# A graph layer on one core: dst broadcast out of SBUF, register loads behind seven columns, fifty double groups without gathers

## The chip, the core and the metric

The kernel runs on one core of one Trainium2 chip. The metric is device time in microseconds of one execution. The kernel before was timed in 13 runs: median 5648.04 us, lowest 5639.12, highest 5659.31. A separate execution was taken with the hardware profiler.

The engines appear under short names: PE is the matrix engine (PEld its weight loads), DVE the vector engine, ACT the scalar engine, POOL the general engine, SP the one that only issues DMAs. Each has a sequencer that reads its instructions in program order. Work of the sequencer itself (register loads, semaphore waits, issuing DMAs) is marked with a q, as in DVEq.

## The reference

One layer of a graph network over 12500 nodes with 128 features and 400000 edges, which are sorted by their destination dst:

```
h   = max(layernorm(x), 0)
m   = relu(concat(h[src], h[dst], edge_attr) @ w1 + b1) @ w2 + b2
agg = segment_sum(m, dst)
out = x + GRU(agg, h)          # gates r, z, n from agg @ w_ih and h @ w_hh
```

All is f32. The heavy part is 400000 rows h[src], taken at random, and a sum by dst.

## The kernel before, in words

**Tables.** A first phase (lines 210 to 337) normalizes x, keeps h transposed in SBUF as hT_all (128 features x 12500 nodes) and writes A = h @ w1[0:128] to DRAM. So an edge needs one row of A, and what depends on dst and the edge's attributes is added by matmuls.

**Units.** The edges come in 3125 tiles of 128. Eight tiles are a double group k (391 of them, 1024 edges each); half of one is a unit u = 2k or 2k+1 (782). All dst of a double group lie in two windows of V = 32 nodes each, since dst is sorted. The main loop (line 932) goes over units, and everything is written out by hand in the order in which each engine is to run it (manual_schedule), with later units' first stages ahead of earlier units' last ones: `stages(u)` (line 896) makes the one-hot of unit u + 6 or so, the matmuls `pre` of unit u + 3, the `add` (L630, DVE) and `relu` (L636, ACT) of unit u + 2, and `seg(u)` (L649, PE) sums unit u by window. Other lines of the loop that matter below, all on DVE: `take` L657 copies a finished sum, `onehot_T` L503 compares the broadcast dst (tile Ld) with the nodes of the window, `window` L522 copies a window's columns of hT_all, `window_rows` L539 adds two windows' rows after PE's L530, and `onehot` L557 makes the one-hot for `seg`.

**Three ways to A's rows.** For most double groups POOL issues eight indirect DMAs (`gather`, L148), each of 128 rows of 512 bytes, into a buffer G. There are GBUFS = 7 buffers after the first stage; the gathers for a later double group are issued when the relu of the second unit has freed one (`gathers`, line 876). The other double groups are "by hand" (SPREAD, line 48): 21 are copied by DVE and 20 by ACT, column by column, out of hT_all (L816 and L814, 128 partitions x 4 bytes each, at an address in a register), and then go through w1 on PE (L616) so that there is no add on DVE; 6 are copied by SP, row by row, from A in DRAM with one DMA of 512 bytes a row (L821). So 1024 columns or rows make one such double group.

**How a job by hand is spread.** `Job` (line 785) loads 32 registers at once (L801, LOAD = 32) with the places of the next 32 columns. DVE and ACT do so once a unit, in `behind` (line 839), which stands right after the add on DVE and right after the relu on ACT: there it runs the columns that are left, TAIL = 9 of them, then loads the next 32 registers. The rest is spread over the four calls of `run_jobs` in the loop, which leave TAIL: with 32 - 9 = 23 columns these are 6, 6 and 6 in phases 1, 2 and 3 of this unit and 5 in phase 0 of the next. Phase 0 stands before `stages`; L539 is issued after phase 3 of an even unit, L557 in `stages` of the odd unit, ahead of its add. A job of DVE or ACT takes at least 32 units (an assert), and jobs of one engine come one after the other over the loop. SP spreads its 1024 DMAs evenly over the units of a job, and its next job begins only when the double group of the last one has been used.

**SP's queue** holds besides these rows the broadcast of dst (`fetch_d`, L496), the edge attributes (`fetch`, L487), index tiles and the nodes' loads and stores. `fetch_d(q)` serves two double groups (QP = 2) and is issued at the head of unit 4q - 12, if one of three buffers of Ld is free.

Of the kernel before, what the change touches and what calls it, by code (L numbers as in the profile page):

```python
# [8 lines left out]
F32 = mybir.dt.float32  # L9
F16 = mybir.dt.float16  # L10
I32 = mybir.dt.int32
# [13 lines left out]
NP = T // PAIR + 1  # L25
NU = 2 * NP

V = 32
# [6 lines left out]
QP = 2  # L35
# [8 lines left out]
CH = PLACE * PAIR  # L44
LOAD = 32

TAIL = 9
SPREAD = {"dve": 21, "act": 20, "sp": 6}
NR = 12672

H_AT = 16512
# [6 lines left out]
def tile_gnn(ctx: ExitStack, tc: tile.TileContext, x, src, srcT, dstT, dstP, eaT, eaP, w1, b1, w2T, b2,  # L58
             wih, bih, whh, bhh, out):
    nc = tc.nc  # L60
# [8 lines left out]
    ge = early.enter_context(tc.tile_pool(name="ge", bufs=EARLY, side="right"))  # L69
# [15 lines left out]

    mode, order = {}, {m: [] for m in SPREAD}
    for m, n in SPREAD.items():
        lo, hi = {"dve": (JOBS0 + 3, NP - 14), "act": (JOBS0 + 11, NP - 6),
                  "sp": (JOBS0 + 5, NP - 10)}[m]
        for i in range(n):  # L90
            k = lo + int((i + 1) * (hi - lo) / n)
# [47 lines left out]
    def gather(k):  # L139
        if k >= NP or k in mode:  # L140
            return
        pool = ge if early_pair(k) else gp
        G[k] = pool.tile([128, GRP, 2, D], F32, name="G")
        table = x if k < RAW else A
        for u in (2 * k, 2 * k + 1):
            for t, j, a in unit_tiles(u):
                c, i = divmod(t, CH)
                nc.gpsimd.indirect_dma_start(  # L148
                    out=G[k][:, j, a, :], out_offset=None, in_=table,
                    in_offset=bass.IndirectOffsetOnAxis(ap=src_i[c][:, i:i + 1], axis=0))  # L150
# [61 lines left out]
    with tc.tile_pool(name="pp", bufs=3) as pp:  # L212
# [69 lines left out]
        def chunk(q):  # L282
            b, c = chunks[q]
            i0, n = bats[b]
            return b, i0, c, min(n, c + 4), PB(b), (i0 + c) * 128
# [3 lines left out]
        for q in range(NC + 3):  # L289
            if q < NC:  # L290
                b, i0, c, e, P, n0 = chunk(q)
# [3 lines left out]
            if 1 <= q <= NC:  # L295
                b, i0, c, e, P, n0 = chunk(q - 1)
# [6 lines left out]
            if q >= 3:  # L303
                b, i0, c, e, P, n0 = chunk(q - 3)
# [4 lines left out]
            if q < NC:  # L309
                b, i0, c, e, P, n0 = chunk(q)  # L310
# [4 lines left out]
            if 1 <= q <= NC:  # L315
                b, i0, c, e, P, n0 = chunk(q - 1)
# [3 lines left out]
            if q >= 3:  # L320
                b, i0, c, e, P, n0 = chunk(q - 3)
                if e == bats[b][1]:
                    nc.sync.dma_start(nodes(A, i0, e, P), asb[b][:P, :e, :])
            if 2 <= q <= NC + 1:
                b, i0, c, e, P, n0 = chunk(q - 2)
# [13 lines left out]
    p3 = ctx.enter_context(tc.tile_pool(name="p3", bufs=3, reuse_waits="tile"))  # L339
# [138 lines left out]
    Ls, Ds, OH, RT, HE, SEG = ({} for _ in range(6))  # L478
    hand = {}

    def fetch(q):
        if q * QP >= NP:
            return
        n = min(QP, NP - q * QP)
        c = slice(q * QP * 512, (q * QP + n) * 512)
        Ls[q] = p3.tile([128, QP * 512], F32, name="L")
        nc.sync.dma_start(Ls[q][2 * V:, :n * 512], eaP[:, c])  # L487

    def fetch_d(q):
        if q * QP >= NP:  # L490
            return
        n = min(QP, NP - q * QP)
        c = slice(q * QP * 512, (q * QP + n) * 512)
        Ds[q] = p3.tile([2 * V, QP * 512], I32, name="Ld")
        for a in range(2):
            nc.sync.dma_start(Ds[q][V * a:V * (a + 1), :n * 512],  # L496
                              dstP[a:a + 1, c].to_broadcast([V, n * 512]))

    def onehot_T(k):
        if k >= NP:  # L500
# [59 lines left out]
    def unit(u):  # L560
        k, h = divmod(u, 2)
        return G[k][:, 2 * h:2 * h + 2, :, :].rearrange("p j a f -> p (j a) f")


    def slots(u):
        return [(j % 2) * 2 + a for _, j, a in unit_tiles(u)]
# [18 lines left out]
    def raw_turn(u):  # L585
        if u < 2 * RAW:
            l = slots(u)
            pt = ps1.tile([128, 512], F32, name="misc")
            for i, s in enumerate(l):
                nc.tensor.transpose(pt[:, i * 128:(i + 1) * 128], unit(u)[:, s, :], ident)  # L590
            hT = p3.tile([128, 512], F32, name="hTe", bufs=2)
            nc.vector.tensor_copy(hT[:, :len(l) * 128], pt[:, :len(l) * 128])
            HE[u] = hT

# [258 lines left out]
    def run_jobs(u, phase):  # L853
# [3 lines left out]
        for m in ("act", "dve"):  # L857
            if m in live:
                n = max(0, len(live[m].vals) - TAIL)
                live[m].run(TAIL + n - -(-n // (4 - PARTS.index(phase))))  # L860
        if phase == 0:
# [14 lines left out]
    def gathers(u):  # L876
        while asked[0] < NP and (asked[0] in mode or 2 * taker[asked[0]] + 1 < u + 2):
            gather(asked[0])
            asked[0] += 1
# [3 lines left out]
            pass  # L883

    gathers(0)
    for q in range(2):
        fetch_d(q)
        fetch(q)
    fetch_d(2)
    for k in range(3):  # L890
        window(k)
# [4 lines left out]
    def stages(u):  # L896
        if u + 7 >= 0:
            raw_stats(u + 7)
        if u + 6 >= 0:
            raw_fin(u + 6)  # L900
            raw_h(u + 6)
        if u % 2 == 0:
            onehot_T(u // 2 + 3)
            if u >= 0:
                window(u // 2 + 3)
        elif u > -7:
            onehot(u // 2 + 3)
        if u + 4 >= 0:
            raw_turn(u + 4)
        if u + 3 >= 0:  # L910
            pre(u + 3)
        if u + 2 >= 0:
            add(u + 2)
            behind("dve", u)
            relu(u + 2)
            behind("act", u)
# [15 lines left out]
    for u in range(NU):  # L932
        k, h = divmod(u, 2)
        gathers(u)
        if h == 0:
            if k % QP == 0:
                fetch_d(k // QP + 3)
                fetch(k // QP + 2)
            if k % BP == 0 and k:
                nodes_left.append([node(k // BP - 1), 0])  # L940
            if k % PLACE == 1:
                indices(k // PLACE + 2)
            if k % PLACE == 5:
                place(k // PLACE + 1)
                dst_tile(k // PLACE + 2)
            if k == NP - 20:
                check_windows()
# [198 lines left out]
```

## Time and profile before

| | us |
|---|---|
| median of 13 runs | 5648.04 |
| lowest, highest | 5639.12, 5659.31 |
| the profiled execution's own time | 5635.89 |
| its span in the trace | 5633.9 |

The first section of the page has busy times and their shares of the span, then the number of instructions:

```profile
PE 3133.0 (56%) x13642; PEld 1881.1 (33%) x13642; DVE 2996.7 (53%) x25579; ACT 2802.7 (50%) x21960; POOL 2626.4 (47%) x2757
```

The queues, with packets, MB and the share of 16 DMA engines' time that the packets took; q0 is POOL's gathers, q1 what SP issues, q14 and q8 the instructions:

```profile
q0 software_dynamic: 87968, 180.33, 12.9%
q1 hardware_dynamic: 68127, 137.35, 8.5%
```

The DMAs that SP issues for dst and the edge attributes, with their number and size:

```profile
Ld<-in_dstP SPq DMA_DIRECT2D x390, 128.0 KB
L<-in_eaP SPq DMA_DIRECT2D x195, 256.0 KB
```

A line of a group of instructions has the source line, engine, operation, out<-in, shapes and number; then busy time and the mean ns of one; then the idle time of the engine just before them and what ended most of it. "issue" there means that no semaphore ended the wait: the sequencer had not got so far. Register loads and DMA issues are not counted as busy. A timeline line has start, length, engine and line; equal instructions that follow one another are merged (x23), and the brackets hold the idle time before the first.

### The profile page before, as it was taken

To read this page: it belongs to the slowest core of one execution; us is meant where nothing else is said; L and a number is where in the kernel's file an instruction comes from. 1 tells how busy PE (TensorE), PEld (TensorE's weight loads), DVE (VectorE), ACT (ScalarE), POOL (GpSimd) and SP (SyncE) were. 2 spreads that over 40 slices of the span, in tenths; PEclk is the share of its full clock that TensorE was granted. 3 is DMA by queue.
4 is the path that set the end of the run, shared out by engine and by line. 5 is a ranking of instruction groups with operands and counts; after the bars stand their busy time and mean duration, and the time that the engine had idled before them with its cause. 6 is when DMAs were issued, how large, how long until landed. Compare 5 with 4: busy or idle time off the path is not lost. (4 is left out here: it accounts for less than half of the span.)

```text
span 5633.9 us, 99560 instructions
## 1 busy us (share of the span) xinstructions
PE 3133.0 (56%) x13642; PEld 1881.1 (33%) x13642; DVE 2996.7 (53%) x25579; ACT 2802.7 (50%) x21960; POOL 2626.4 (47%) x2757
## 2 busy tenths in 40 slices
PE   2665555455556555545655554555555456465557
PEld 2532333333323333323333332333333233233334
DVE  3645555555555555555555555555555555555553
ACT  2413554546454554545455545555454545455454
POOL 5445444444444444454444444453444444444443
PEclk7775666566566666656657665666666666566667
DMA  3322222221222222221222222222222222222221
GB/s 111 82 63 60 56 57 57 57 56 51 58 56 57 57 55 55 53 59 48 57 57 52 58 54 56 55 54 56 54 53 58 56 54 53 58 56 54 58 53 46
DMA packets 156906, 324.15 MB, mean 58 GB/s; under 512 B 64549, under 2 KB 76624, under 8 KB 156239
## 3 DMA queue, kind: packets, MB, share of 16 engines
q0 software_dynamic: 87968, 180.33, 12.9%
q1 hardware_dynamic: 68127, 137.35, 8.5%
q14 instruction: 553, 4.53, 0.3%
q8 instruction: 114, 1.87, 0.1%
q10 hardware_dynamic: 144, 0.07, 0.0%
HBM read 303.66 MB, written 13.84 MB: 56 GB/s over the span
## 5 line engine op out<-in xcount | busy, mean ns | idle before, releaser
L148 POOL DMA_INDIRECT G<-A,src_i x2672 | 2552.4, 955 | 2929.2 <-ACT RB L636 2056.2
L814 ACT COPY HE_act<-hT_all 128x4 uint8 x20480 | 2237.0, 189 | 1583.7 <-issue 1568.6
L816 DVE TENSOR_REDUCE HE_dve<-hT_all 128x4 uint8 x21504 | 1700.6, 147 | 1817.6 <-issue 1807.0
L605 PE MATMUL pre<-RW,L 128*128 128x256 f32 x3128 | 1383.6, 581 | 1376.0 <-DVE G L630 1170.7
L605 PEld LDWEIGHTS pre<-RW,L 128*128 128x128 f32 x3128 | 806.8, 286 | 1758.9 <-issue 1382.0
L636 ACT ACTIVATE RB<-G 128x512 f32<-128x512 f32 x668 | 420.2, 629 | 694.8 <-DVE G L630 350.6
L530 PE MATMUL oh<-w1b,hw 128*64 128x128 f32 x782 | 242.5, 408 | 865.0 <-DVE hw L522 461.3
L649 PE MATMUL seg<-RB,OH 128*32 128x129 f32 x6250 | 704.7, 365 | 10.8 <-ACT RB L636 6.3
L630 DVE TENSOR_TENSOR G<-pre,G 128x512 f32<-128x512 f32 x668 | 456.8, 684 | 58.7 <-issue 45.6
L649 PEld LDWEIGHTS seg<-RB,OH 128*32 128x32 f32 x6250 | 377.6, 140 | 279.8 <-issue 157.7
L530 PEld LDWEIGHTS oh<-w1b,hw 128*64 128x64 f32 x782 | 102.7, 186 | 1075.5 <-DVE hw L522 566.0
L539 DVE TENSOR_TENSOR RW<-oh,b1b 32x128 f32<-32x128 f32 x782 | 217.0, 277 | 311.2 <-issue 209.1
L658 ACT CAST dcol<-seg 64x1 f16<-64x1 f32 x391 | 59.6, 152 | 315.3 <-DVE sums L657 145.0
L657 DVE COPY sums<-seg 64x128 f32<-64x128 f32 x391 | 107.5, 275 | 199.4 <-remote 118.7
L503 DVE TENSOR_SCALAR L<-Ld,node_of 64x512 f32<-64x512 int32 x391 | 186.8, 478 | 2.6 <-issue 2.6
L557 DVE TENSOR_TENSOR OH<-dloc,iota 128x256 f32<-128x256 f16 (+1 forms) x392 | 162.8, 416 | 1.1 <-issue 0.2
L680 PE MATMUL nd<-spot,sums 64*128 64x40 f32 x782 | 157.6, 386 | 1.0 <-issue 1.0
L680 PEld LDWEIGHTS nd<-spot,sums 64*128 64x128 f32 x782 | 153.4, 301 | 12.0 <-issue 12.0
L644 PE MATMUL seg<-zrow 1*64 1x129 bf16 x391 | 114.2, 292 | 0.9 <-remote 0.9
L699 PE MATMUL misc<-DEG,brow 33*128 33x512 f32 x112 | 72.7, 732 | 67.0 <-DVE gt L716 67.0
L328 PE MATMUL pre<-w1a,hT_all 128*128 128x128 f32 x196 | 51.5, 415 | 77.7 <-issue 58.0
L699 PE MATMUL nd<-DEG,brow 33*128 33x512 f32 x112 | 89.0, 886 | 3.8 <-ACT HE_act L814 2.5
(151 smaller groups left out, 1726.9 us busy)
## 6 DMA issues: line engine op xcount, KB each, us to landing
G_sp<-A SPq DMA_DIRECT2D x6144, 0.5 KB
Ld<-in_dstP SPq DMA_DIRECT2D x390, 128.0 KB
L<-in_eaP SPq DMA_DIRECT2D x195, 256.0 KB
G<-A,src_i POOLq DMA_INDIRECT x2672
xb<-in_x SPq DMA_DIRECT2D x28, 256.0 KB
out<-xb SPq DMA_DIRECT2D x28, 256.0 KB
xs<-in_x SPq DMA_DIRECT2D x11, 512.0 KB
A<-asb SPq DMA_DIRECT2D x11, 512.0 KB
```

The costliest lines, as they stand in the source:

```text
L148: nc.gpsimd.indirect_dma_start(out=G[k][:, j, a, :], out_offset=None, in_=table, in_offset=bass.IndirectOffsetOnAxis(ap=src_i[c][:, i:i + ...
L503: nc.vector.tensor_scalar(Ls[k // QP][:2 * V, c], Ds[k // QP][:, c], node_of[:, k:k + 1], None, op0=ALU.is_equal)
L530: nc.tensor.matmul(PB_[k][:2 * V, :D], HW.pop(k).rearrange("p a v -> p (a v)"), w1b, start=True, stop=True)
L539: nc.vector.tensor_tensor(RW[k % 4][s, a, :], pm[s, :D], b1b[s, :], op=ALU.add)
L557: nc.vector.tensor_tensor(o, d.to_broadcast(shape), i.to_broadcast(shape), op=ALU.is_equal)
L605: nc.tensor.matmul(PP[u][:, 2 * i:2 * i + 2, :], Ls[k // QP][:, c0:c0 + 128], RW[k % 4], start=True, stop=not raw)
L630: nc.vector.tensor_tensor(RT[u], PP.pop(u), RT[u], op=ALU.add)
L636: nc.scalar.activation(o[:, :, :D], RT.pop(u), AF.Relu)
L649: nc.tensor.matmul(SEG[k][V * a:V * (a + 1), :D + 1], OH[k][:, j, a, :], RB[u % 3][:, (j % 2) * 2 + a, :D + 1], start=False, stop=all(b != ...
L680: nc.tensor.matmul(pt[:, bass.ds(offs[i], V + SHIFT)], sums[:, i, :], spot, start=False, stop=i == n - 1)
L814: nc.scalar.copy(to[:, e * 4:e * 4 + 4], h_bytes[:, bass.ds(v - H_AT, 4)])
L816: nc.vector.tensor_reduce(to[:, e * 4:e * 4 + 4], h_bytes[:, bass.ds(v - H_AT, 4), None], AX.X, ALU.max)
```

## The change

Three edits, in one diff (its core):

```diff
-TAIL = 9
-SPREAD = {"dve": 21, "act": 20, "sp": 6}
+TAIL = 7
+SPREAD = {"dve": 22, "act": 21, "sp": 7}
...
+    DST = 64
+    dst_s = {}
+
+    def stage_dst(c):
+        n = min(DST, NP - c * DST)
+        if n <= 0:
+            return
+        dst_s[c] = p3.tile([128, 512], I32, name="dst_s", bufs=2)
+        for a in range(2):
+            nc.sync.dma_start(dst_s[c][DST * a:DST * a + n, :],
+                              dstP[a:a + 1, c * DST * 512:(c * DST + n) * 512].rearrange(
+                                  "o (k e) -> (o k) e", e=512))
...
     def fetch_d(q):
         if q * QP >= NP:
             return
-        n = min(QP, NP - q * QP)
-        c = slice(q * QP * 512, (q * QP + n) * 512)
+        if q * QP % DST == DST // 2:
+            stage_dst(q * QP // DST + 1)
         Ds[q] = p3.tile([2 * V, QP * 512], I32, name="Ld")
-        for a in range(2):
-            nc.sync.dma_start(Ds[q][V * a:V * (a + 1), :n * 512],
-                              dstP[a:a + 1, c].to_broadcast([V, n * 512]))
+        for k in range(q * QP, min(NP, (q + 1) * QP)):
+            for a in range(2):
+                r = DST * a + k % DST
+                nc.sync.dma_start(
+                    Ds[q][V * a:V * (a + 1), (k % QP) * 512:(k % QP + 1) * 512],
+                    dst_s[k // DST][r:r + 1, None, :].to_broadcast([1, V, 512]))
...
-            hT = p3.tile([128, 512], F32, name="hTe", bufs=2)
+            hT = ge.tile([128, 512], F32, name="hTe", bufs=2)
...
     gathers(0)
+    stage_dst(0)
```

First, dst of 64 double groups is loaded at a time into a tile of 128 partitions (one half of a double group's dst in each partition, 512 numbers or 2 KB), 32 double groups ahead. The broadcast to 32 partitions then reads one partition of that tile in place of DRAM; it is one DMA of 64 KB for each half of a double group, four for two double groups, where there were two of 128 KB. The tile hTe of the first units moves to another pool, which is closed later on.

Second, nine columns behind the add and the relu become seven, so 25 are left for the four phases: 7, 6 and 6 in phases 1 to 3 and 6 in phase 0.

Third, 22, 21 and 7 double groups are copied by DVE, ACT and SP, 50 in place of 47, and 24 gathers fewer are issued by POOL. The jobs' spans become shorter: 32 or 34 units for most of DVE's (34 before), 34 for ACT's (36 before), and some 94 for SP's (110 before).

## The prediction

> **What bounds the kernel now.** I read the groups first, then a timeline of DVE, ACT and POOL over one pair of units, then the register loads by line, then SP's waits.
>
> ```profile
> L148 POOL DMA_INDIRECT G<-A,src_i x2672 | 2552.4, 955 | 2929.2 <-ACT RB L636 2056.2
> L814 ACT COPY HE_act<-hT_all 128x4 uint8 x20480 | 2237.0, 189 | 1583.7 <-issue 1568.6
> L816 DVE TENSOR_REDUCE HE_dve<-hT_all 128x4 uint8 x21504 | 1700.6, 147 | 1817.6 <-issue 1807.0
> ```
>
> No engine is busy for more than 56% of the span. POOL's largest idle time ends with a relu (L636), which is what frees a G buffer. DVE and ACT idle before their columns for "issue": they wait for nothing that a semaphore shows. The timeline, with lines left out, says what that is:
>
> ```profile
> 3041.95 0.63 ACT L636 ACTIVATE RB<-G 128x512 f32<-128x512 f32 x1
> ...
> 3042.45 1.56 DVE L816 TENSOR_REDUCE HE_dve<-hT_all 128x4 uint8 x23 [0.68 <-issue]
> ...
> 3042.84 0.95 POOL L148 DMA_INDIRECT G<-A,src_i  x1 [5.99 <-ACT RB L636]
> ...
> 3044.62 0.66 DVE L816 TENSOR_REDUCE HE_dve<-hT_all 128x4 uint8 x9
> ...
> 3046.35 0.29 DVE L816 TENSOR_REDUCE HE_dve<-hT_all 128x4 uint8 x3 [1.08 <-issue]
> ...
> 3049.25 0.16 DVE L816 TENSOR_REDUCE HE_dve<-hT_all 128x4 uint8 x1 [0.51 <-issue]
> ...
> 3051.59 0.95 POOL L148 DMA_INDIRECT G<-A,src_i  x1 [0.30 <-issue]
> ...
> 3054.26 0.35 DVE L816 TENSOR_REDUCE HE_dve<-hT_all 128x4 uint8 x4 [0.57 <-issue]
> 3054.52 0.56 DVE L539 TENSOR_TENSOR RW<-oh,b1b 32x128 f32<-32x128 f32 x2
> ```
>
> A relu frees a buffer; 0.9 us later POOL issues eight gathers, 1.25 us apart (0.95 busy and 0.30 between). While their data is on the way, columns that ran 64 ns apart come one or two in 0.7 us, on ACT and SP too, and it ends about 0.5 us after the last gather has landed, which is 1.26 us after POOL's last instruction. Then DVE runs its leftover columns, L539 twice, the columns of phase 0, L557 and the add; ACT does the relu, and the next burst starts. So a pair of units (one double group) with gathers lasts 0.9 + 9.7 + 1.3 + 0.5 us, plus the leftover, plus 2.2 us from L539 to the relu. Sorting the relus by start, 293 pairs with a full burst took 15.0 us in the mean, and 43 pairs without a gather 9.5 us. DVE's program between the end of the slow stretch and the relu sets the end; ACT waits for the add.
>
> Before each stretch of columns stands a load of 32 registers, and it is not cheap:
>
> ```profile
> L801 DVEq TENSOR_LOAD <-at x672: 2097/2122/2834, 358.3 to 5453.8; - x168
> L801 ACTq TENSOR_LOAD <-at x640: 1965/2004/2491, 470.6 to 5558.2; - x160
> ```
>
> The columns issued ahead of it (nine) are what DVE does meanwhile; then it idles 0.89 us in the mean (0.79 on ACT).
>
> **The sum's base.** The profiled execution took 5635.9 us, its span 5633.9; the median of the 13 runs is 5648.0, so I add 12.1 at the end.
>
> **Three more double groups without gathers.** Three pairs go from 15.0 to 9.5 us: -16.5. DVE gets 1024 columns more, in 32 units or 16 pairs, some 14 of them with a burst. There, a pair has 8 leftover columns (mean) and 5 of phase 0 between the slow end and the add: 13 x 64 ns = 0.83 us, x14 = +12; the other columns lie under the burst. ACT gets 16 pairs more with columns. 32 pairs without them took 14.49 us with 7.8 gathers, 259 with them 14.37 with 6.9; at 5.5/8 = 0.69 us a gather that is 0.5 us a pair, x16 = +8. Adds, seven columns' matmuls and the like of three groups are under 5 us on engines that wait; nothing.
>
> SP gets 1024 copies more, 0.32 us apart in calm stretches and 0.56 in the mean, and 32 loads of 2.1: 400 to 640 us. Its waits:
>
> ```profile
> SPq L496 <- DVE hw L522: 435.6, 88, 32.2
> SPq L821 <- ACT RB L636: 90.4, 5, 22.2
> SPq L487 <- PE seg L649: 50.0, 18, 7.3
> ```
>
> With the smaller ones some 700 us are free while jobs run. SP reaches the fetch of a unit about 28 us before DVE reaches that unit, and a landed Ld waits 55 to 75 us for its use. I take nothing for SP; the other end is below.
>
> **Loads behind 7 columns, not 9.** In 307 of the 672 DVE loads (those of odd units) the load starts 22 ns after the add starts, with nine columns still to come, and in 27 others 49 ns after the instruction before L557, with L557 and nine to come: the sequencer could not run further ahead. With two fewer behind it, the odd unit's load should start about when L557 does, 0.42 + 0.03 us before the add. Relative to the add it then starts 0.46 us earlier, but the two columns are done later: -0.46 + 0.13 = -0.33 us to the next unit's L657. In the even unit the load starts 0.12 us after L503 starts, and could start some 0.3 us earlier until the sequencer's own pace (48 ns an instruction) holds it. So that load ends 0.33 us earlier against the burst. What is this worth? Loads that end 3 to 4 us into a burst are followed by 13.5 columns before the first gap, at 4 to 5 us by 8.3, at 5 to 6 us by 5.0: 3.3 to 5.2 columns a us, so 1.1 to 1.7 columns or 0.07 to 0.11 us. Against it stand one more column behind the load (25 in four parts is 7, 6, 6, 6 where 23 was 6, 6, 6, 5) and one more in phase 0: +0.13. Net +0.04 in each of some 270 pairs: +11. In 46 pairs without a burst both loads count, with two columns given back: -0.33 + 0.13 = -0.2 each: -9.
>
> From both sides: if no load starts sooner, two columns lose their cover at each load, 0.26 us a pair, x316 = +81; if all of both gains counted in every pair, -0.66 + 0.19, x270 = -127. I take +2 since the rows of columns after a load are the nearest.
>
> **dst out of SBUF.** Two DMAs for two double groups become four; the two of a staging come once in 64 groups. Issue: L496 takes 0.37 us (median), 390 more are 145 us on SP, in the same free time. DVE's L503 now has up to two more semaphores to wait for: a sequencer wait takes 70 ns of its pace, 196 x 2 x 0.07 = 27 at most, ahead of the even unit's load. I take +7. The first fetch must wait for the staging: some 3 us at 173 us, where the first L503 comes at 186.9 and has no DMA to wait for; nothing. hTe's move changes only where it lies. The transfer: today 128 packets of 2 KB take 0.1 us each on 16 engines. No row reads one partition from 16 engines. Below: the same 0.1 us, and no gain either, since neither gathers (1.26 us to landing, 1.38 at the 95th of 100, with or without Ld) nor L503 wait for it. Above: one engine's row of 512 bytes into one partition is 27 ns, 19 GB/s; if the partition gives only that to all, 64 KB take 3.4 us, four DMAs 14 us of each 28.5, and a packet 1.7 us. A gather packet behind one lands that much later: half of 293 pairs x 1.7 = +249 at most. I take 0: the load is 6 groups ahead of its use and 16 queues' packets overlapped from one DRAM row.
>
> [...]
>
> Sum: -16.5 + 12 + 8 + 11 - 9 + 7 = +12.5, so 5648.4 in the profile and **5660** as a median.
>
> **Rivals.**
> - *The loads are worth more* (faster). If columns saved from the slow stretch also save what stalls behind them, a pair with a burst gains 0.2 us, about half of the bound above: -54 in place of +11, total -52: 5596. For it: 1807 us of "issue" on DVE is the largest idle time. Against: most of it lies under a burst.
> - *dst crowds the gathers* (slower). The partition's 14 us in 28.5 cover a burst's end in half of the pairs, and half a packet, 0.85 us, is the mean delay: 293 x 0.5 x 0.85 = +125, or 5785. It decides from the point where a 2 KB packet takes over 0.5 us. SP's shortage has the same sign: 640 + 67 + 190 against 700 free is up to 200 us, if its new copies fall into slow stretches.
> - *TAIL does not do what it says*: the sequencer is not held by what is queued, and nothing starts earlier: +81 for +2, 5739.
>
> **Chances.** Forecast (the edits cancel, 5640 to 5680) 0.36; loads worth more 0.34; dst or SP late 0.20; no earlier load 0.10. A measurement tells 0.2% (11 us) from nothing. Faster is the first rival and a little of the forecast's own width, 0.38; half of the forecast is within 0.2%, 0.18; slower is the rest, 0.44. The forecast's own range is 5640 to 5680; the range to hold 8 in 10 takes in the first rival and most of the third and cuts the second: 5585 to 5760.
>
> **What would show it.** Pairs with a burst at 15.0 us; DVE's loads starting at L557 rather than the add; the idle time before L816 per load down from 0.89 or up; the Ld packets' time in the queue table; gathers' landing still 1.26 us after POOL's last; SP still waiting at the fetch of dst. I am wrong if pairs with a burst shorten by 0.2 us or more, if landing moves, or if SP's wait is gone and DVE waits at L503.

## The result, and the profile after

The changed kernel took 5907.97 us (median of 8 runs, 5897.48 to 5930.09) where the kernel before took 5647.87 in 37 runs: a ratio of 1.0467, 95% interval 1.0455 to 1.0478, or 260 us more. The forecast was 5660, with 5760 as the upper end.

The changed kernel's page, first the busy time by engine, then the two queues and the DMAs for dst and the edge attributes, then the three groups. Lines of the code lie 16 or 17 further down than before (L496 is now L512, L605 L622, L636 L653, L801 L818, L816 L833, L821 L838).

```profile
PE 3131.1 (53%) x13674; PEld 1878.8 (32%) x13674; DVE 3055.6 (52%) x26599; ACT 2902.0 (49%) x22984; POOL 2614.4 (44%) x2733
...
q1 hardware_dynamic: 89889, 139.52, 17.8%
q0 software_dynamic: 87200, 178.76, 11.6%
...
L148 POOL DMA_INDIRECT G<-A,src_i x2648 | 2540.5, 959 | 3204.8 <-ACT RB L653 2315.8
L831 ACT COPY HE_act<-hT_all 128x4 uint8 x21504 | 2323.0, 189 | 1721.9 <-issue 1697.6
L833 DVE TENSOR_REDUCE HE_dve<-hT_all 128x4 uint8 x22528 | 1765.0, 147 | 2028.3 <-issue 2018.6
...
Ld<-dst_s SPq DMA_DIRECT2D x782, 64.0 KB
L<-in_eaP SPq DMA_DIRECT2D x195, 256.0 KB
```

Busy time hardly moved: DVE has 59 us more, ACT 99, POOL 12 less. The 260 us are waiting. POOL waits 260 us more for a relu, so the pairs became longer: 15.6 us with a burst (15.0 before) and 10.9 without (9.5). Queue q1 moved 1.6% more bytes but its packets took twice the time, 17.8% for 8.5%. The packet records say which: 33294 packets of 2 KB at 393 ns in the mean, 782 x 32 of them the broadcasts out of SBUF. In a fetch with no other 2 KB packets beside it these take 490 ns in the mean: 42% of them 84 ns or little more, 37% over 800 ns, and 99 in 100 under 1.12 us.

SP's waits in the changed kernel (what was waited for, total us, times, longest):

```profile
SPq L512 <- DVE hw L539: 71.6, 11, 23.0
...
SPq L838 <- ACT RB L653: 20.6, 6, 5.2
...
SPq L487 <- PE seg L666: 2.8, 7, 1.0
```

Before, these were 435.6, 90.4 and 50.0. SP's spare time is nearly gone. And PE has a wait in the changed kernel that was not in its list before, the third here:

```profile
PE pre L622 <- DVE G L647: 920.4, 191, 8.9
PE oh L547 <- DVE hw L539: 410.5, 162, 11.3
PE pre L622 <- DMA L<-in_eaP: 402.3, 43, 18.2
```

L is the edge-attribute tile. A timeline of the changed kernel (start, length, engine, line) shows one such wait, all engines in one window, with lines left out:

```profile
3376.20 11.63 SPq L838 DMA_DIRECT2D G_sp<-A  x18
...
3378.75 1.07 PE L666 MATMUL seg<-RB,OH 128*32 128x129 f32 x8
...
3387.92 3.15 SPq L512 DMA_DIRECT2D Ld<-dst_s  x4
...
3391.17 0.54 SPq L487 DMA_DIRECT2D L<-in_eaP  x1
...
3397.09 1.19 PE L622 MATMUL pre<-RW,L 128*128 128x256 f32 x2 [17.26 <-DMA L<-in_eaP]
```

PE has been idle since 3379.8. SP is still issuing rows of its own job, then the four copies of dst, and gets to L at 3391.2; L lands some 5 us later. I followed SP's lead (time from its issue of Ld at the head of a unit to DVE's L520 of that unit) through the run: before it is 27 us in the mean and never under 12; after, it falls in each of the seven SP jobs from some +17 us to between -30 and -45 in about 100 units, 0.6 us a unit, and recovers when the job ends.

So the first theories were: **A**, SP's queue has become the bound; **B**, the copies out of SBUF themselves hold up other transfers; **C**, the shorter TAIL or the added columns cost it.

### The profile page after: what moved, and what is told of

It is laid out like the page before. It is cut to its first block, busy times and chain, and to the rows that moved or that the text cites. A ratio compares the mean times of both kernels' runs of the same rounds, so it can differ in the third digit from the quotient of the medians.

```text
span 5898.6 us, 104372 instructions
## 1 busy us (share of the span) xinstructions
PE 3131.1 (53%) x13674; PEld 1878.8 (32%) x13674; DVE 3055.6 (52%) x26599; ACT 2902.0 (49%) x22984; POOL 2614.4 (44%) x2733
## 3 DMA queue, kind: packets, MB, share of 16 engines
q1 hardware_dynamic: 89889, 139.52, 17.8%
## 5 line engine op out<-in xcount | busy, mean ns | idle before, releaser
L831 ACT COPY HE_act<-hT_all 128x4 uint8 x21504 | 2323.0, 189 | 1721.9 <-issue 1697.6
L833 DVE TENSOR_REDUCE HE_dve<-hT_all 128x4 uint8 x22528 | 1765.0, 147 | 2028.3 <-issue 2018.6
L622 PE MATMUL pre<-RW,L 128*128 128x256 f32 x3128 | 1369.6, 576 | 1570.4 <-DVE G L647 920.4
L622 PEld LDWEIGHTS pre<-RW,L 128*128 128x128 f32 x3128 | 798.8, 283 | 1957.2 <-issue 1637.5
L653 ACT ACTIVATE RB<-G 128x512 f32<-128x512 f32 x662 | 416.4, 629 | 606.2 <-DVE G L647 279.1
L520 DVE TENSOR_SCALAR L<-Ld,node_of 64x512 f32<-64x512 int32 x391 | 187.4, 479 | 5.3 <-issue 5.1
L539 DVE COPY hw<-hT_all 128x64 f32 x391 | 78.9, 202 | 27.6 <-issue 17.2
```

What stands on the lines that cost most here:

```text
L520: nc.vector.tensor_scalar(Ls[k // QP][:2 * V, c], Ds[k // QP][:, c], node_of[:, k:k + 1], None, op0=ALU.is_equal)
L622: nc.tensor.matmul(PP[u][:, 2 * i:2 * i + 2, :], Ls[k // QP][:, c0:c0 + 128], RW[k % 4], start=True, stop=not raw)
L653: nc.scalar.activation(o[:, :, :D], RT.pop(u), AF.Relu)
L831: nc.scalar.copy(to[:, e * 4:e * 4 + 4], h_bytes[:, bass.ds(v - H_AT, 4)])
L833: nc.vector.tensor_reduce(to[:, e * 4:e * 4 + 4], h_bytes[:, bass.ds(v - H_AT, 4), None], AX.X, ALU.max)
```

## The experiments

Each ratio is to the kernel before on the experiment's own chip, with its 95% interval. On those chips the kernel before took 5559 to 5560 us (the first two groups and b_sp1, b_none11), 5637 (b_spread, a_l_act, b_sp5, b_half) and 5622 (a_l4, h_sbuf, b_few, b_act). Names with a_ start from the changed kernel, with b_ from the one before; h_sbuf is b_half with dst out of SBUF.

### One edit taken back

a_sp6: six SP jobs.

```diff
-SPREAD = {"dve": 22, "act": 21, "sp": 7}
+SPREAD = {"dve": 22, "act": 21, "sp": 6}
```

> The changed kernel with six SP jobs in place of seven; dst still comes from SBUF in four DMAs a fetch, and TAIL is 7. Theory A (SP's queue has become the bound: within each SP job it falls behind by about 60 us in 100 units, 0.6 us a unit, and TensorE then waits for L): with 9.3 copies a unit for 11 SP has 1.0 us a unit more, keeps its lead of 15 to 30 us, the wait of L622 on L's DMA (402 us) falls under 60 us, and the time is 5650 to 5720 us. Theory B (the broadcasts out of SBUF themselves, with packets of 393 ns, hold up gathers and L): the packets are as before, so the wait stays above 250 us and the time above 5800 us. Theory C (the shorter TAIL and the longer columns cost it): above 5800 us also, without a wait for L.

Measured 1.0244 (1.0221 to 1.0267). The wait for L is gone and SP's lead is 26 us, as A said; but over half of the loss stays, as A did not.

a_dram2: `fetch_d` as before the change; a_dram4: the same, but in four DMAs, so that only the source differs from the change.

```diff
-                    dst_s[k // DST][r:r + 1, None, :].to_broadcast([1, V, 512]))
+                    dstP[a:a + 1, k * 512:(k + 1) * 512].to_broadcast([V, 512]))
```

> The changed kernel with dst out of DRAM again, in two DMAs of 128 KB a fetch; TAIL 7 and the 22, 21 and 7 jobs stay. Theory A: SP is spared two issues of about 0.85 us in four units, 0.4 us a unit of the 0.6 that it loses, so it still loses ground inside each SP job but little of it reaches TensorE: 5650 to 5740 us, wait for L under 120 us. Theory B: all of the loss goes, 5620 to 5680 us, and SP's lead is as in the kernel before. Theory C: above 5800 us.

> The changed kernel with dst out of DRAM, but in the same four DMAs of 64 KB and packets of 2 KB as the change has; only the source of the copy differs from the changed kernel. Theory A in its form 'number of issues': SP's issues are as many, so SP falls behind as in the changed kernel and the time stays at 5850 to 5930 us. Theory B: packets at about 100 ns in place of 393, so the time falls to 5640 to 5720 us. Halfway, 5740 to 5850 us, would say that the issue of a copy out of SBUF is itself longer on SP.

Measured 1.0176 (1.0159 to 1.0193) and 1.0182 (1.0165 to 1.0199). The number of DMAs costs nothing that can be measured; the source costs some 2.9%. From DRAM the 2 KB packets take 107 ns and an issue 0.36 us of SP (mean), from SBUF 393 ns and 0.68 us.

a_tail9: the changed kernel with TAIL = 9.

> The changed kernel with TAIL 9 again, nothing else. Theories A and B: SP's queue and the broadcasts are as they were, so the time stays within 1% of 5908 us (5850 to 5960 us) and the wait for L at 300 to 500 us. Theory C: the loads in the midst of the columns were the cost, and the time falls below 5780 us.

Measured 1.0488 (1.0460 to 1.0516): C falls for TAIL.

The expectations of these four count in us for a chip on which the kernel before takes 5648. There the four ratios stand for 5786, 5747, 5751 and 5924 us. So a_sp6 lies between A and B, a_dram2 a little above both, a_dram4 in the halfway band (an issue out of SBUF is indeed longer), and a_tail9 where A and B put it. No single theory holds; the rest takes the edits one by one.

### One edit made alone

b_sbuf has the hunks of the change for `stage_dst`, `fetch_d` and hTe, and the constants of before. The other three change a constant of the kernel before each, in the order b_sp7, b_tail7, b_cols:

```diff
-SPREAD = {"dve": 21, "act": 20, "sp": 6}
+SPREAD = {"dve": 21, "act": 20, "sp": 7}
...
-TAIL = 9
+TAIL = 7
...
-SPREAD = {"dve": 21, "act": 20, "sp": 6}
+SPREAD = {"dve": 22, "act": 21, "sp": 6}
```

> The kernel before with one part of the change: dst is copied out of SBUF (with hTe in its other pool, which makes the room), TAIL 9 and 21, 20 and 6 jobs as before. Theory A (the broadcasts cost only SP's time, and only where SP runs out of it): with six SP jobs the changed kernel kept a lead of 26 us, so nothing reaches TensorE, ratio 0.997 to 1.004. Theory B (the broadcasts also hold up the gathers' landing and the L tiles): ratio 1.006 to 1.015, with gathers landing later than 1.26 us after POOL's last instruction in a quarter of the bursts.

> The kernel before with seven SP jobs in place of six, dst out of DRAM, nothing else. Theory A: SP's lead over VectorE falls from 27 to some 10 us on the mean, but never far enough that TensorE waits for L; one pair less has a burst (5.5 us saved), ratio 0.997 to 1.003. Against it: the copies of rows lengthen the pairs by 0.04 to 0.06 us each, some 2.5 more a pair, ratio 1.006 to 1.010.

> The kernel before with TAIL 7 in place of 9, nothing else. The prediction took +2 us, bounds -127 and +81 us. From the changed kernel with 7 and with 9 (1.0467 and 1.0488, intervals that meet): ratio 0.996 to 1.003. If the shorter tail hurts without the rest, 1.005 to 1.015.

> The kernel before with 22 VectorE jobs and 21 ScalarE jobs in place of 21 and 20, six SP jobs, TAIL 9, dst out of DRAM. The prediction's working (two pairs without a burst save 11 us; a tenth more columns cost 20 us): ratio 1.000 to 1.003. Theory D (columns cost more than their busy time, since they and their loads lie in the stretch in which the gathers slow the sequencers): the changed kernel with dst out of DRAM is 1.018 with 7 SP jobs, and most of that is the columns, ratio 1.010 to 1.018.

Measured:

| edit alone | ratio | 95% interval | us |
|---|---|---|---|
| dst out of SBUF | 1.0173 | 1.0146 to 1.0199 | 96 |
| seventh SP job | 1.0111 | 1.0082 to 1.0139 | 62 |
| TAIL 7 | 1.0015 | 0.9999 to 1.0030 | 8 |
| 22 and 21 jobs on DVE and ACT | 1.0075 | 1.0047 to 1.0104 | 42 |

TAIL came as expected. dst out of SBUF and the seventh job lie a little above the upper range of each, the columns between their two ranges. In none of the four does PE wait for L for more than 11 us (b_sp7). SP's lead in b_sp7 is 2.5 us in the mean, but inside a job it falls from 17 us or more to between -10 and -30 (means of five fetches), with dst out of DRAM. So the seventh job alone takes SP out of its time. The three sizable ones add up to 3.6%; the changed kernel with TAIL 9 has just these three, on chips of the same speed, and costs 4.9%. Pairs of edits without that surplus fit the sum: a_sp6 has 2.4 where the parts give 2.6, a_dram2 1.8 where they give 2.0. So the surplus shows only where the SBUF copies and the seventh job meet (always with the added columns too; the two alone were not run).

**Where b_sbuf loses it.** The q1 lines of b_sbuf and a_dram4:

```profile
q1 hardware_dynamic: 87835, 138.98, 18.7%
```

```profile
q1 hardware_dynamic: 88901, 137.92, 8.5%
```

A fetch of 128 packets takes 5.5 us from the first start to the last end in b_sbuf, 2.1 in a_dram4 (medians). I took each burst of eight gathers and asked when its last packet ended after POOL's last instruction. With no L or dst packets near the burst's end, it is 1.24 us in b_sbuf and 1.25 in a_dram4. With them, in 105 of 299 bursts of b_sbuf, 2.21 us in the mean; in a_dram4, 37 bursts, 1.48 us. A third of b_sbuf's bursts land later than 1.5 us (kernel before: 4%). This moves the landing by 0.3 us in the mean, or 90 us over 300 bursts, a little of which comes back, because columns run in the meantime.

### Three mechanisms, tried apart

b_spread: b_sbuf with each row on four partitions, 32 apart (and 16 double groups staged at a time in eight DMAs, 200 in all where the expectation says 100; these lines are left out here).

```diff
-                    dst_s[k // DST][r:r + 1, None, :].to_broadcast([1, V, 512]))
+                    dst_s[k // DST][r:r + 97:32, None, :].to_broadcast([4, V // 4, 512]))
```

> The kernel before with dst copied out of SBUF (TAIL 9, 21, 20 and 6 jobs), but every row lies on four partitions, 32 apart, and each of the same 64 KB copies reads a quarter from each; 16 pairs are staged at a time, 100 stagings in all. Theory B1 (one partition feeds all 32 packets of a copy, so that its 2 KB packets take 391 ns in place of 107, a fetch takes 5.5 us in place of 2.1, and the gathers of a third of the bursts land 1 us later): packets of 100 to 200 ns, landing over 1.5 us in under 15% of the bursts, ratio 1.001 to 1.008. Theory B2 (a copy out of SBUF is slow whatever partition it reads): packets above 330 ns and ratio 1.014 to 1.020, as in the kernel with the single row.

Measured 1.0180 (1.0163 to 1.0197). Packets fell to 111 ns and late landings to 10%, as B1 said, but the time did not follow. The test was not clean: 4 to 6 packets were in flight at a time where b_sbuf has 16 or 17, so a fetch still took 4.6 us; and SP's lead fell to 13 us with the stagings' DMAs. It says that shorter packets alone don't help, and not which partition arrangement would. It also speaks against the landing as the whole cost: its cycles, counted as in the table further down, are 15.4 us where the kernel before, on a chip of the same speed, has 15.1; the landing is 1.35 us (before 1.29), but the next burst comes 4.3 us after it (before 4.0). This loss lies behind the landing, and what makes it is not shown.

a_l_act: the changed kernel with L on ScalarE's queue.

```diff
-        nc.sync.dma_start(Ls[q][2 * V:, :n * 512], eaP[:, c])
+        nc.scalar.dma_start(Ls[q][2 * V:, :n * 512], eaP[:, c])
```

> The changed kernel with the edge-attribute tile L fetched from ScalarE's queue, no longer behind SP's copies; nothing else. Theory A for the part of the loss that the single parts don't give (they add to 3.7%, the change costs 4.7%): L arrives late only because SP issues it late, so the wait of L622 on L's DMA (402 us) falls under 60 us, and the ratio to 1.033 to 1.041. If the transfer of L itself is what is late, the wait stays above 250 us and the ratio above 1.044. ScalarE's own issue of 196 copies is some 0.5 us each, beside its columns.

Measured 1.1073 (1.1036 to 1.1111): neither. By the profile, ACT itself now stood 970 us ahead of its columns (L831) until DMAs that SP issues had ended. It settles nothing on L.

a_l4: L two pairs earlier instead.

```diff
-        Ls[q] = p3.tile([128, QP * 512], F32, name="L")
+        Ls[q] = p3.tile([128, QP * 512], F32, name="L", bufs=4)
...
-                fetch(k // QP + 2)
+                fetch(k // QP + 3)
```

> The changed kernel with L fetched two pairs (some 30 us) earlier into four buffers; the room comes from one buffer of dst_s (staged at the start of its 64 pairs), one of hTe and four of OH in place of six. Theory A (the loss beyond the added parts is TensorE's wait for L, because SP issues it late): the wait of L622 on L's DMA falls from 402 us to under 60, the ratio from 1.047 to 1.033 to 1.041. If the wait goes and the ratio stays at 1.044 or more, the wait for L only took the place of another wait, and SP's lateness reaches the pairs by another way (the rows of G_sp, or dst itself).

Measured 1.0435 (1.0415 to 1.0454). PE's wait for L is gone entirely, but only 0.3% of the time with it (on chips whose speed differs by 0.5%, and with fewer buffers for OH, dst_s and hTe, which may cost something of their own). The instructions on tile Ld in a_l4 say what is late next: DVE's line L520, which compares dst, now stands for it.

```profile
L520 DVE TENSOR_SCALAR L<-Ld,node_of x391: 464/479/717, 186.6 to 5831.8; 64x512 f32<-64x512 int32 x196
its engine sat idle before it (us, times) until:
  DMA Ld<-dst_s: 72.9, 18
```

17 of these 18 waits fall into four stretches of 8 to 12 double groups, where SP's lead is lowest. SP is still 11 us behind DVE in the mean, and whatever it issues is late in turn. The 402 us of waiting were thus worth about 20 us of time; of the rest, 196 us are back as PE's wait for DVE's add, which rose from 920 to 1116.

h_sbuf: dst out of SBUF with 11, 10 and 3 jobs, to be set against b_half below.

> The kernel before with 11, 10 and 3 jobs and dst copied out of SBUF, TAIL 9; to be set against the same with dst out of DRAM (0.9447), in which SP waits 1530 us at the fetch of dst. Theory landing (the 2 KB packets of 391 ns stand ahead of the gathers' last packets; a third of the bursts land 1 us later, some 350 bursts, 0.3 us each, 100 us): ratio 0.957 to 0.966. Theory SP (the copies cost SP's time, which is to spare here): ratio 0.943 to 0.949, with a third of the bursts landing late all the same.

Measured 0.9541 (0.9520 to 0.9563) against 0.9447: 1.0% for the copies, while SP waits over 1200 us at their fetch:

```profile
SPq L512 <- DVE hw L539: 1257.2, 124, 35.3
```

34% of the bursts land later than 1.5 us, 0.26 us in the mean over the cycles below, and these cycles are 0.26 us longer (14.11 to 14.37). The ratio lies between the two expected ranges, but these two numbers agree: where SP has time, the copies cost about what they add to the landing. That is a match of two means; b_spread, which cost as much with few late landings, does not fit it.

### Do pairs by hand pay at all?

b_sp7 and b_cols had asked what one more job costs. These ask what fewer bring. Each is one line of the kernel before, in the order b_sp5, b_half, b_few, b_act, b_sp1:

```diff
-SPREAD = {"dve": 21, "act": 20, "sp": 6}
+SPREAD = {"dve": 21, "act": 20, "sp": 5}
+SPREAD = {"dve": 11, "act": 10, "sp": 3}
+SPREAD = {"dve": 1, "act": 1, "sp": 1}
+SPREAD = {"dve": 1, "act": 20, "sp": 1}
+SPREAD = {"dve": 21, "act": 20, "sp": 1}
```

> The kernel before with five SP jobs in place of six. If a seventh job costs 1.1% because every row copy lengthens the pair by 0.05 us (1024 copies, 51 us, against 5.5 us for a pair without a burst), the same holds for the sixth, and this is faster: ratio 0.988 to 0.996. If it cost 1.1% only because SP ran short of time (its lead fell from 27 us to 2.5), then five give back a pair with a burst and nothing else: ratio 1.000 to 1.003.

> The kernel before with 11 VectorE, 10 ScalarE and 3 SP jobs in place of 21, 20 and 6, so that 23 more pairs have a burst. If columns and copies cost more than they save at any number (VectorE's column 0.04 us, ScalarE's 0.01, a row copy 0.05, by a fit over the pairs): 10 * 41 + 10 * 10 + 3 * 51 less 23 * 5.5 is some 500 us saved, ratio about 0.91. If they are free up to about the number that the kernel before has, only the 23 bursts come back: ratio 1.020 to 1.025.

> The kernel before with one job of each kind in place of 21, 20 and 6, so that 44 more pairs than before have a burst. If jobs cost more than they save at any number (in the kernel with half of them the pairs without columns took 11.8 us, with VectorE's 14.1 to 14.6): 388 pairs of 11.8 us and 490 us around them, some 5070 us or 0.90. If POOL becomes the bound (8 gathers of 1.22 us are 9.8 us, and 1.25 us to land and some 3 us to the next burst make 14 us a pair): 0.96 to 0.98, a little slower than with half.

> The kernel before with ScalarE's 20 jobs, one of VectorE and one of SP, so that 25 more pairs have a burst. By the fit over the pairs (ScalarE's column 0.01 us, so a job costs 10 us and saves 5.5 to 12): 0.90 to 0.93, like the kernel with three jobs or a little faster. By the pairs of the kernel with half of the jobs (ScalarE's columns alone 13.6 us, none 11.8): 244 of 369 pairs at 13.6 and the rest at 11.8, 0.95 to 0.965 of the time before.

> The kernel before with one SP job in place of six, 21 VectorE and 20 ScalarE jobs as before; five more pairs have a burst. If a row copy costs 0.05 us wherever SP stands (1024 copies, 51 us, less 5.5 to 15 us for the pair's burst, as the sixth job's 0.45% and the seventh's 1.1% suggest): 25 to 60 us a job, ratio 0.95 to 0.978. If copies cost only where SP runs short of time, five bursts come back: 1.003 to 1.008.

| jobs DVE, ACT, SP | ratio | 95% interval |
|---|---|---|
| 21, 20, 5 | 0.9955 | 0.9938 to 0.9971 |
| 21, 20, 1 | 0.9708 | 0.9692 to 0.9724 |
| 11, 10, 3 | 0.9447 | 0.9429 to 0.9466 |
| 1, 20, 1 | 0.9187 | 0.9172 to 0.9202 |
| 1, 1, 1 | 0.8902 | 0.8886 to 0.8918 |

Every step down is faster than the kernel before, as the first expectation of each had it (b_half by 60% of its amount), and the kernel with three jobs beats both kernels: 5003.6 us against 5622.5 before on its chip. POOL issues 352 gathers more in it and waits far less. Its groups' first line, and POOL's waits:

```profile
L148 POOL DMA_INDIRECT G<-A,src_i x3024 | 2881.6, 953 | 1944.1 <-issue 873.1
```

```profile
POOL G L148 <- ACT RB L636: 505.0, 104, 15.2
POOL G L148 <- ACT dcol L658: 437.8, 99, 6.7
```

Before, POOL waited 2056 us for a relu. Over the 344 pairs of the main stretch, the mean pair takes 12.4 us in b_few and 14.3 in the kernel before, although 43 pairs of the latter have no burst.

The cycle from one burst's first instruction to the next one's shows how jobs lengthen it (own means over the full bursts of each trace, us and numbers):

| kernel | cycle | last instruction to landing | landing to next burst | DVE columns in the burst, after landing | rows of SP in the burst |
|---|---|---|---|---|---|
| b_act | 13.46 | 1.25 | 2.33 | 3.0, 0.8 | 2.4 |
| b_sp1 | 14.32 | 1.26 | 3.28 | 44.0, 14.8 | 2.0 |
| b_tail7 | 14.84 | 1.25 | 3.78 | 41.7, 17.4 | 8.2 |
| b_sp7 | 15.05 | 1.25 | 4.02 | 37.6, 21.8 | 10.6 |
| b_sbuf | 15.00 | 1.56 | 3.67 | 38.8, 19.6 | 8.2 |
| after | 15.62 | 1.44 | 4.37 | 38.2, 21.9 | 9.6 |

b_act has one job of DVE and shows the cycle without its columns. In the five kernels with 21 or 22 such jobs, the more rows SP copies during a burst, the fewer columns DVE gets done in it, and on the whole the more are left after the landing and the later the next burst (b_sbuf, with as many rows as b_tail7, has fewer columns and yet an earlier burst; the two differ in TAIL too). That is a correlation over five kernels; through what the rows slow DVE, no run shows.

b_none11: no job at all, and the room of the jobs as four more gather buffers throughout (what prepares the jobs' indices is left out).

```diff
+SPREAD = {"dve": 0, "act": 0, "sp": 0}
...
-        return k < EARLY or EARLY + GBUFS <= k < 2 * EARLY + GBUFS
+        return k % (EARLY + GBUFS) < EARLY
```

> No pair by hand at all; the room of their buffers stays with the gathers, which have eleven buffers from start to end in place of seven after the first 15 pairs. Theory 'jobs cost more than they save at any number': faster than with three jobs (0.890), and with the four more buffers POOL's wait on the relu (505 us with three jobs) falls, ratio 0.86 to 0.885. If some other stage than the gathers is now the bound, 0.887 to 0.892, the same as with three jobs.

Measured 0.9027 (0.9012 to 0.9042), 5013.6 us against 5558.9 on its chip, which neither range holds. In microseconds that is b_few's time, so the last three jobs and the four buffers decide nothing. That kernel before differs by 1.1% between the two chips and these two don't is a warning: ratios from chips of different speed are comparable to about 1% only.

## Why the prediction was wrong, step by step

- **Three pairs without a burst, -16.5, and 1024 columns on DVE, +12, on ACT, +8.** For DVE and ACT (two of the pairs) that made about +9; measured 42. The failed step is "15.0 us with a burst, 9.5 without". Both were means over pairs that carry 60 columns of DVE, 57 of ACT and 17 rows of SP. A pair with a burst and without such columns takes about 12.4 us, not 15 (the mean of the same 344 pairs is 12.4 in b_none11, which has no job, and in b_few; the 95 pairs of b_half without a column take 12.6). The saving was taken from loaded pairs, and the price of the load was counted in a few columns after the landing alone, not in those that the burst no longer covers.
- **SP's copies and loads, 0.** Measured 62 us with dst out of DRAM. "700 us free" was a sum over the run; inside a job the time was not there (lead down to between -10 and -30 us), though PE waited only 11 us for L. And the copies were not free while they were in time either: the sixth job cost 25 us (b_sp5) and the second to the sixth together 163 us (b_sp1), some 33 each, the saved bursts already taken off. So about half of the 62 is what any such job costs; that the rest is SP's shortage is argued, not shown. The other end named, up to +200 for SP's shortage, had the sign.
- **TAIL, +2.** Measured +8, interval -1 to +17. The size was right by two errors. "The odd unit's load should start about when L557 does" failed: in the changed kernel 92% of 306 such loads start 15 to 60 ns after the add starts (median 19), as 82% did before, now with seven columns to come. It is not the number of queued instructions that holds it there. The even unit's load did start earlier, by some 0.3 us. Idle per DVE load went from 0.89 to 0.91 us in b_tail7.

```profile
L818 DVEq TENSOR_LOAD <-at x704: 2097/2149/9692, 358.3 to 5722.5; - x176
L818 ACTq TENSOR_LOAD <-at x672: 1966/2020/6489, 473.8 to 5821.3; - x168
```

  (These are the loads of the changed kernel. A load's median is as before; its maximum of 2.8 us has become 9.7.)
- **dst out of SBUF, transfer 0, waits +7.** Measured 96 us: the largest mis-sized term. "16 queues' packets overlapped from one DRAM row", so also from one partition, was the wrong row to lean on. The rival came near it: it decided from a packet of 0.5 us, and the copies' packets took 0.49 in the mean, over a third of them about 1 us; "half of 293 bursts, 0.85 us each" became a third, 1 us each. That the 96 us are these late landings is supported by h_sbuf and not by b_spread. The prediction also read the dst packets of before as 128 of 2 KB; by the difference between the packet records they are 64 of 4 KB a fetch.
- **The upper bound, four copies in 14 us.** Measured: 256 KB out of four rows in 5.5 us (median, in b_sbuf and in the changed kernel), 48 GB/s over the four where the bound took 19 GB/s for one row after the other; a packet at 0.49 us in the mean where it took 1.7; and 96 us where it took 249 at most. What sets the 5.5 us no run shows: b_spread, whose copies read four partitions each, had short packets (111 ns), but its 4.6 us came with 4 to 6 of them in flight.
- **No interaction.** The prediction priced SP's shortage and the SBUF packets as one rival, each alone. The edits share SP's queue: a unit has 11 rows in place of 9.3, which alone exceeds the unit (b_sp7), and an issue out of SBUF takes 0.3 us more, which takes the lowest lead from between -10 and -30 us to between -30 and -45. That surplus is 1.3% (4.9 for 3.6, with an uncertainty of half a per cent). PE's wait for L is 0.3% of it by a_l4; that the rest is dst and rows coming late is argued from SP's lead and the new wait at L520, not shown.

What was to be seen: pairs with a burst at 15.0, seen 15.6; landing at 1.26, seen 1.44 in the cycles' mean; SP still waiting at the fetch, seen 72 us of 436. The text's own signs for being wrong, that landing moves and SP's wait goes, both came; the wait stood at PE for L, and at DVE's L503 (now L520) only once L was taken care of.

## What to carry to other kernels

The average pair is not the marginal pair: before adding to a scheme, take some of it away; one run with three jobs would have shown that the other 44 cost 619 us more than they saved. A row in the trace that shares the form but not the source (DRAM at 107 ns a packet, not SBUF at 393) prices nothing; where the bounds are +0 and +249 us and no row decides between them, the forecast belongs between the bounds. And when a queue's lead is what hides two edits, add their demands before calling either free.

## What the runs showed of the hardware

- A broadcast of one SBUF partition by DMA (the changed kernel): a 2 KB packet takes from 0.08 us to 1.12 (99 in 100), 0.49 in the mean with 15 to 18 in flight at a fetch's peak (out of DRAM 0.11, a_dram4); 256 KB in four copies take 5.5 us, from DRAM 2.1 (a_dram4).
- SP's issue of such a copy takes 0.58 us (median), with one source partition (the changed kernel) or four (b_spread); out of DRAM 0.41 for the same size (a_dram4).
- b_spread's copies, with 4 in the slowest dimension, had 4 to 6 packets in flight; b_sbuf's, with 32, had 16 or 17. Whether the dimension or the four partitions make the difference, no run shows.
- In most odd units DVE's register load starts some 20 ns after the add: 92% of them with seven columns behind the add (median 19 ns, the changed kernel), 82% with nine (the kernel before).
